# A transformer layer with FP4 feed-forward on one core: FP4 and layer norm in steps of different periods, and the queue's part between the two pairs of maxima

## The chip, the core and the metric

The kernel runs on one core of one Trainium2 chip. The metric is the device time of one execution in microseconds; of the kernel before, three executions took 3696.54, 3698.85 and 3699.21 us, median 3698.85. Five engines work side by side, each through its own instruction stream: TensorE (PE in the profile; PEld is its loading of weights), VectorE (DVE), ScalarE (ACT), GpSimd (POOL) and SyncE (SP), which in this kernel issues nearly all DMAs. They wait for each other through semaphores only.

## What is computed

A post-norm transformer layer over 4 batches of 2048 rows of 256 numbers: attention with 16 heads of 16, and a gated feed-forward of 704 columns whose linears take inputs and weights rounded to FP4 in blocks of 16.

```python
def fp4_quant_dequant(x):                  # blocks of 16 along the last dim
    scale = jnp.maximum(jnp.max(jnp.abs(xb), axis=-1, keepdims=True) / 6.0, 1e-12)
    idx = jnp.searchsorted(_MID, jnp.abs(xb / scale))
    return (_GRID[idx] * jnp.sign(xb) * scale).reshape(shape)
def fp4_linear(x, w):
    return jnp.einsum('bsk,nk->bsn', fp4_quant_dequant(x), fp4_quant_dequant(w))

scores = jnp.einsum('bhld,bhmd->bhlm', q, k) * SCALE
out = jnp.einsum('bhlm,bhmd->bhld', softmax(scores), v)      # then @ Wo.T
x = layernorm(x + attention(x))
h = silu(fp4_linear(x, w_gate)) * fp4_linear(x, w_up)
x = layernorm(x + fp4_linear(h, w_down))
```

## The kernel before

**Steps and periods.** The attention is cut into 64 steps, one for each batch `b`, block of 512 queries `qb` and group `g` of four heads (two pairs). A step has 16 periods, one for each 128 keys; the main loop (L700 to L736) runs over 1046 periods. Three steps are in the works at once: in one period, `maxima` (L382) makes the scores of one step for 128 queries against 512 keys, only to find each row's maximum; 20 periods later (`LEAD`) `exponentials` (L423) makes the transposed scores of that step again, the maxima subtracted inside the matmul, and takes the exponential; 2 periods after that (`LAG`) `values` (L434) multiplies by V.

**A period before, in TensorE's order:** two pairs of `pm` matmuls (one pair for each pair of heads; each fills one of two PSUM buffers of pool `ps_m`, and VectorE's `mx` reduction at L397 reads that buffer and frees it); two `pe` matmuls with two exponentials on ScalarE (L431); four `av`; the other two `pe` with their exponentials; at the end, `period(1)` (L654).

**The queue.** All other work is cut into parts by generators: a `yield` of 300 (`LEAST`) or more ends a part, of less it goes on. `period` first runs the steps that are due (`take_due`, L122), then one part of each generator in `urgent` (`max_rows`, which turns a finished step's maxima into rows for Q; `normalize`, which divides by the sums), and if none of these was a part, one part of `queue`. The queue holds the projections (`project`, L300: transposes of `xb`, then `pq` matmuls for K and Q, `pv` for V; order of the pieces at L666), the preparation of the weights (`prepare`, L232), and for each finished block of 512 queries a `chain` with the output projection and the feed-forward (L585), in which the next batch's projection (`other`) is threaded. PSUM for the parts and for `pe` comes in turn from the three banks of `ps_x`.

**A chain (four steps, 64 periods):** `residual` (four `py` parts, GpSimd adds, layer norm, FP4), seven parts of `other` (L596), transposes of the rounded rows (`ptq`), `gate(0)`, two of `other`, `gate(1)`, two, `gate(2)`, two (a gate is four parts: `pg`, `pu`, `pg`, `pu`, each product on GpSimd), `turned` for tiles 0 and 1 (transposes `pth` of the rounded `h`), `gate(3)`, the rest of `other`, `down` (eight parts `pz` in two tiles), layer norm of the output rows, `turned` for 2 and 3, `down`. In the last chain the gates of odd tiles run on VectorE. A generator whose input isn't ready yields `LEAST`, so its period has no part.

**FP4** (`fp4`, L145): VectorE takes each block's largest (`amax`, L149), the scale (`sc`, L151) and its reciprocal (`rs`, L153); GpSimd (or the engine given) makes `xn` (L155, L157). A period later, through `later`, VectorE makes the power of two (`m`, L161, L162), and GpSimd adds and takes it away again and multiplies by the scale (L163 to L165). **Layer norm** (L484): `st` and `mv` on VectorE for two row tiles (L489, L490), the rest on GpSimd (L492 to L497).

**What sets the order.** TensorE's instructions stay in the order written (`keep_in_program_order`). On the other engines a scheduler orders instructions as their data become ready, program order deciding among those that are; so VectorE's small instructions can stand in another place than where the code puts them.

**Loads.** `load_k` (L365) brings K tiles of 512 keys from DRAM into one of 20 buffers, each issued every four periods a step and more ahead; `xnh` has three buffers and holds Q, K, V weights at the start and later the FP4 values of `h`.

Of the kernel before, what the change touches and what calls it, by code (L numbers as in the profile page):

```python
# [73 lines left out]
def block_kernel(  # L74
# [36 lines left out]


    clock = {"now": 0}
    due = deque()

    def later(periods, step, rest=0):

        state = {"done": None}
        due.append((clock["now"] + periods, step, state))
        return lambda: state["done"] is not None and clock["now"] >= state["done"] + rest  # L120

    def take_due():  # L122
        clock["now"] += 1
        for _ in range(len(due)):
            at, step, state = due.popleft()
            if at > clock["now"]:
                due.append((at, step, state))
                continue
            step()
            state["done"] = clock["now"]  # L130


    def matmul(*args, **kw):
        tc.keep_in_program_order(nc.tensor.matmul(*args, **kw))  # L134
# [9 lines left out]

    def fp4(pool, t, tag, gain=1.0, engine=None):  # L145

        p, nb, _ = t.shape
        amax = pool.tile([p, nb], F32, tag="amax" + tag, name="amax")
        nc.vector.tensor_reduce(amax, t, AX.X, ALU.max, apply_absolute_value=True)  # L149
        sc = pool.tile([p, nb], F32, tag="sc" + tag, name="sc")  # L150
        nc.vector.tensor_scalar(sc, amax, gain / 6.0, 1e-12, ALU.mult, ALU.max)  # L151
        rs = pool.tile([p, nb], F32, tag="rs" + tag, name="rs")
        nc.vector.reciprocal(rs, sc)  # L153
        engine = engine or nc.gpsimd
        engine.tensor_scalar(rs, rs, gain * TIES_DOWN, 1.0, ALU.mult, ALU.mult)  # L155
        xn = pool.tile([p, nb, FB], F32, tag="xn" + tag, name="xn", bufs=3 if tag else 2)
        engine.tensor_tensor(xn, t, rs.unsqueeze(2).to_broadcast([p, nb, FB]), ALU.mult)  # L157

        def rounded():
            m = pool.tile([p, nb, FB], F32, tag="m" + tag, name="m", bufs=1)  # L160
            nc.vector.tensor_single_scalar(m.bitcast(I32), xn.bitcast(I32), EXPONENT, ALU.bitwise_and)  # L161
            nc.vector.tensor_scalar(m, m, 1.0, ROUND, ALU.max, ALU.mult)  # L162
            engine.tensor_tensor(xn, xn, m, ALU.add)  # L163
            engine.tensor_tensor(xn, xn, m, ALU.subtract)  # L164
            engine.tensor_tensor(xn, xn, sc.unsqueeze(2).to_broadcast([p, nb, FB]), ALU.mult)  # L165

        return xn, later(1, rounded, 4 if tag == "" else 2)

# [36 lines left out]
    for name, w in (("wk", wk), ("wq", wq), ("wv", wv)):  # L205
        loaded[name] = p2.tile([P, KC, D], F32, tag="xnh", name=name, bufs=3)
        nc.scalar.dma_start(loaded[name], w.rearrange("(c p) k -> p c k", p=P))
# [24 lines left out]
    def prepare():  # L232
# [12 lines left out]
        def load(w, i):  # L245
            if w is w_down:
                t = p2.tile([P, FF], F32, tag="wl", name="wl", bufs=1)
                nc.sync.dma_start(t, w[i * P : (i + 1) * P, :])
                return fp4(p2, t.rearrange("p (b f) -> p b f", f=FB), "h")
            t = p2.tile([RF, 2, D], F32, tag="wl", name="wl", bufs=1)  # L250
            nc.sync.dma_start(t, w[2 * i * RF : 2 * (i + 1) * RF, :].rearrange("(c p) k -> p c k", p=RF))
            return fp4(p2, t.rearrange("p c (b f) -> p (c b) f", f=FB), "")

        def transposed(w, i, q, done):
            while not done():
                yield LEAST
            if w is w_down:
                q = q.rearrange("p b f -> p (b f)")
# [41 lines left out]
    def project(b, tb, what):  # L300
# [7 lines left out]
        for kc in range(KC):  # L308
# [4 lines left out]
            yield 600  # L313
        for name, c in [(w[0], int(w[1])) for w in what if w != "v"]:
            w, dst = (wkT, kx[b % 2][c][:, :, rows]) if name == "k" else (wqT, qx[(b * NQB + tb) % len(qx)][c])
# [16 lines left out]
            projected.add((b, tb, name + str(c)))  # L332
        for t in range(QT if "v" in what else 0):
            v = vt[t // 2]
            pv = psum("pv")
            for kc in range(KC):
                matmul(
                    pv[:, :D], xT[:, kc, t * P : (t + 1) * P], wvT[:, kc, :], start=(kc == 0), stop=(kc == KC - 1)
                )
            src = pv[:, :D].rearrange("p (g i j d) -> p g i j d", g=NG, i=NP, j=2)  # L340
            for j in range(2):
                nc.scalar.copy(v[:, :, t % 2, :, 2 * j * DH : (2 * j + 1) * DH], src[:, :, :, j, :])
            if t % 2:
                t0 = tb * QT + t - 1
                for g in range(NG):
                    nc.sync.dma_start(vx[b % 2][g, :, t0 : t0 + 2, :], v[:, g].rearrange("p t i c -> p t (i c)"))
            if t == QT - 1:
                projected.add((b, tb, "v"))
            yield 900

# [14 lines left out]
    def load_k(s, kb):  # L365
        b, qb, g = steps[s]
        for i in range(NP):
            c, h = divmod(g * HG + i * 2, NC)
            k = p1.tile([P, QB], F32R, tag="k", name="k", bufs=20)
            for j in range(2):  # L370
                nc.sync.dma_start(
                    k[R * j : R * j + R, :].bitcast(F32), kx[b % 2][c][:, h + j, kb * QB : (kb + 1) * QB]
                )
            k_sb[s, i, kb] = k
# [108 lines left out]

    def layer_norm(r, t0, n):  # L484

        mv = p2.tile([P, n, 2], F32, tag="mv", name="mv")
        for t in range(n):
            st = p2.tile([P, 6], F32, tag="st", name="st")
            nc.vector.bn_stats(st, r[:, t0 + t, :])  # L489
            nc.vector.bn_aggr(mv[:, t, :], st)  # L490
        rstd = p2.tile([P, n], F32, tag="rstd", name="rstd")
        nc.gpsimd.tensor_scalar_add(rstd, mv[:, :, 1], LN_EPS)  # L492
        nc.gpsimd.tensor_tensor(rstd, rstd, minus_half[:, :n], ALU.pow)
        minus = p2.tile([P, n], F32, tag="minus", name="minus")
        nc.gpsimd.tensor_scalar(minus, mv[:, :, 0], -1.0, 1.0, ALU.mult, ALU.mult)
        for t in range(n):
            nc.gpsimd.tensor_scalar(  # L497
                r[:, t0 + t, :], r[:, t0 + t, :], minus[:, t : t + 1], rstd[:, t : t + 1], ALU.add, ALU.mult
            )

    def residual(b, qb, x1, xq):

        for t in range(QT):
# [10 lines left out]
            if t % 2:  # L514
                layer_norm(x1, t - 1, 2)
                tiles = x1[:, t - 1 : t + 1].rearrange("p t (b f) -> p (t b) f", f=FB)
                later(3, lambda tiles=tiles: xq.append(fp4(p2, tiles, "")))
            yield 900
# [35 lines left out]
    def turned(hq, tiles, hT):  # L554

        while not all(t in hq and hq[t][1]() for t in tiles):
            yield LEAST
        hq = [hq[t][0].rearrange("p b f -> p (b f)") for t in tiles]
        for t in range(2):
# [25 lines left out]
    def feed_forward(b, qb, between):  # L585
# [9 lines left out]
        other = projection(*between) if between is not None else iter([LEAST] * 6)  # L595
        yield from islice(other, 7)  # L596
        while len(xq) < QT // 2 or not all(done() for _, done in xq):
            yield LEAST
        xqT = p1.tile([P, KC, QB], F32, tag="xqT", name="xqT")
        for kc in range(KC):  # L600
            pt = psum("ptq")
            for t in range(QT):
                q = xq[t // 2][0].rearrange("p (t b) f -> p t (b f)", t=2)
                transpose(pt[:, t * P : (t + 1) * P], q[:, t % 2, kc * P : (kc + 1) * P], ident)
# [4 lines left out]
        def gate(t):  # L609
# [3 lines left out]
            yield from gated(xqT, h, t, engine)  # L613
            blocks = h.rearrange("p (b f) -> p b f", f=FB)
            later(1, lambda: hq.update({t: fp4(p2, blocks, "h", gain=0.5, engine=engine)}))

        def out_rows(t):
            layer_norm(x1, t, 2)
            at = slice(qb * QB + t * P, qb * QB + (t + 2) * P)
            nc.sync.dma_start(out[b, at, :].rearrange("(t p) d -> p t d", p=P), x1[:, t : t + 2, :])  # L620

# [4 lines left out]
        yield from gate(2)  # L626
        yield from islice(other, 2)
        hT = p2.tile([P, 2, NFC, P], F32, tag="hT", name="hT", bufs=1)
        yield from turned(hq, (0, 1), hT)
        yield from gate(3)  # L630
        yield from other
# [68 lines left out]
    for n in range(-LEAD, N + LAG):  # L700
# [10 lines left out]
        if n > 0 and kt % QT == 0:  # L711
            ahead, kb = divmod(n - QT + 2 * NKT, NKT)
            if ahead < len(steps):
# [6 lines left out]
                load_k(ahead, kb // QT)  # L720

        for i in range(NP):
            if m < N:
                maxima(sm, im, i)
        for i in range(NP):
            if 0 <= n < N:
# [5 lines left out]
        if n >= LAG and kv == NKT - 1:  # L732
            urgent.append(normalize(sv))
            if sv % NG == NG - 1:
                queue.append(chain(*steps[sv][:2]))
        period(1 if n >= 0 else 2)  # L736
    banks["more"] = True
# [37 lines left out]
```

## Time and profile before

| what | us |
|---|---|
| median of three executions | 3698.85 (3696.54 to 3699.21) |
| the profiled execution, its time | 3695.37 |
| its span in the profile | 3693.6 |
| TensorE busy | 3540.7 |
| VectorE busy (of it maxima, L397) | 2805.0 (2407.9) |
| ScalarE busy (of it exponentials, L431) | 2694.0 (2217.9) |
| GpSimd busy | 1293.4 |

The clock granted to TensorE was 0.982 of full speed over the whole span. By stretches, TensorE's busy time was:

| stretch, us | TensorE busy, us | of us |
|---|---|---|
| 0 to 100 | 63.01 | 100 |
| 100 to 330 | 201.05 | 230 |
| 330 to 500 | 168.14 | 170 |
| 500 to 3500 | 2963.06 | 3000 |
| 3500 to 3600 | 95.78 | 100 |
| 3600 to 3694 | 49.70 | 94 |

How the views below are read. In a line of the groups, after the bar stand busy time, mean nanoseconds of one, and after the second bar the engine's idle time just before those instructions with what ended it. A line of the waits says who waited for whom: microseconds in total, times, longest. A line of a timeline has start, duration, engine, line, operation, output and inputs with the shape, and in brackets the idle time just before it. A matmul is called by its output: `pm` are scores for maxima, `pe` for exponentials.

### The profile page before, as it was taken

To read this page: it belongs to the slowest core of one execution; us is meant where nothing else is said; L and a number is where in the kernel's file an instruction comes from. 1 tells how busy PE (TensorE), PEld (TensorE's weight loads), DVE (VectorE), ACT (ScalarE), POOL (GpSimd) and SP (SyncE) were. 2 spreads that over 40 slices of the span, in tenths; PEclk is the share of its full clock that TensorE was granted. 3 is DMA by queue.
4 is the path that set the end of the run, shared out by engine and by line. 5 is a ranking of instruction groups with operands and counts; after the bars stand their busy time and mean duration, and the time that the engine had idled before them with its cause. 6 is when DMAs were issued, how large, how long until landed. Compare 5 with 4: busy or idle time off the path is not lost.

```text
span 3693.6 us, 57860 instructions
## 1 busy us (share of the span) xinstructions
PE 3540.7 (96%) x21396; PEld 1602.0 (43%) x21396; DVE 2805.0 (76%) x3250; ACT 2694.0 (73%) x5452; POOL 1293.4 (35%) x1542
## 2 busy tenths in 40 slices
PE   5889999999999999999999999999999999999995
PEld 4433444444444444444444444444443434444343
DVE  3777777787787877878787787778778788878834
ACT  2667777777777777777777777777777777777772
POOL 0331432424243242423424243342424325241425
PEclk8899999999999999999999999999999999999997
DMA  6643333223232332323323232322322221222100
GB/s 217 188 137 117 93 91 105 81 85 115 68 114 84 94 94 85 109 70 109 95 78 106 85 97 88 97 89 74 113 75 63 75 79 57 75 68 86 47 7 6
DMA packets 197954, 334.18 MB, mean 90 GB/s; under 512 B 26024, under 2 KB 75560, under 8 KB 197672
## 3 DMA queue, kind: packets, MB, share of 16 engines
q1 hardware_dynamic: 196280, 329.16, 29.2%
q8 instruction: 171, 2.80, 0.3%
q10 hardware_dynamic: 1392, 1.31, 0.1%
q14 instruction: 111, 0.91, 0.1%
HBM read 242.81 MB, written 86.51 MB: 89 GB/s over the span
## 4 chain that ended last, share of the span: by engine, by line
PE 82%; DVE 11%; DMA 2%; POOL 2%; SPq 1%; issue 1%; ACT 1%; ACTq 0%; POOLq 0%; DVEq 0%
PE av L134 24%; PE pe L134 18%; PE pm L134 16%; DVE mx L397 8%; PE pz L134 5%; PE pg L134 5%; PE pu L134 5%; PE pq L134 3%; PE pth L137 1%; PE pv L134 1%; PE pa L137 1%; PE py L134 1%; PE pn L137 1%; DMA k<-kx 1%; DMA xb<-in_L_attn_x_dram 1%; DVE amax L149 1%
## 5 line engine op out<-in xcount | busy, mean ns | idle before, releaser
L397 DVE TENSOR_REDUCE mx<-pm 128x2 f32<-128x1024 f32 x2048 | 2407.9, 1217 | 706.8 <-PE pm L134 702.5
L431 ACT ACTIVATE e<-pe 128x512 f32<-128x512 f32 x4096 | 2217.9, 595 | 671.2 <-PE pe L134 666.0
L134 PE MATMUL av<-e,v 128*32 128x512 f32 x8192 | 1098.3, 608 | 0.0
L134 PE MATMUL pe<-q,k 64*128 64x512 f32 x4096 | 1037.2, 456 | 4.8 <-ACT e L431 4.4
L134 PEld LDWEIGHTS pe<-q,k 64*128 64x128 f32 x4096 | 476.4, 185 | 969.0 <-ACT e L431 855.7
L134 PE MATMUL pm<-k,q 62*128 62x512 f32 x4096 | 803.8, 448 | 60.0 <-DVE mx L397 53.0
L134 PEld LDWEIGHTS pm<-k,q 62*128 62x128 f32 x4096 | 347.0, 186 | 373.2 <-issue 178.6
L134 PEld LDWEIGHTS av<-e,v 128*32 128x32 f32 x8192 | 162.2, 108 | 332.2 <-issue 314.1
L537 POOL TENSOR_TENSOR a<-a,g 128x352 f32<-128x352 f32 x124 | 116.4, 939 | 499.5 <-ACT a L536 499.5
L582 POOL TENSOR_TENSOR x<-x,read 128x128 f32<-128x128 f32 x128 | 58.9, 460 | 493.6 <-ACT read L142 493.6
L134 PE MATMUL pz<-wdT,hT 128*128 128x128 f32 (+1 forms) x1536 | 230.0, 292 | 0.0
L163 POOL TENSOR_TENSOR xn<-xn,m 128x704 f32<-128x704 f32 (+2 forms) x104 | 159.5, 1534 | 157.7 <-DVE m L162 139.0
L134 PEld LDWEIGHTS pz<-wdT,hT 128*128 128x128 f32 (+1 forms) x1536 | 191.0, 191 | 45.5 <-ACT e L431 18.2
L551 POOL TENSOR_TENSOR h<-a,u 128x352 f32<-128x352 f32 x124 | 116.2, 937 | 226.7 <-ACT u L550 224.4
L134 PE MATMUL pg<-wgT,xqT 128*128 128x352 f32 x512 | 187.4, 489 | 0.0
L513 POOL TENSOR_TENSOR x<-x,read 128x256 f32<-128x256 f32 x64 | 46.7, 730 | 400.2 <-ACT read L142 399.9
L134 PE MATMUL pu<-wuT,xqT 128*128 128x352 f32 x512 | 186.1, 486 | 0.0
L164 POOL TENSOR_TENSOR xn<-xn,m 128x704 f32<-128x704 f32 (+2 forms) x104 | 159.8, 1536 | 5.6
L165 POOL TENSOR_TENSOR xn<-xn,sc 128x704 f32<-128x704 f32 (+2 forms) x104 | 131.5, 1264 | 7.8
L538 POOL TENSOR_TENSOR a<-a,g 128x352 f32<-128x352 f32 x124 | 118.8, 958 | 9.7
L134 PEld LDWEIGHTS pg<-wgT,xqT 128*128 128x128 f32 x512 | 88.3, 191 | 58.5 <-ACT e L431 19.1
L134 PEld LDWEIGHTS pu<-wuT,xqT 128*128 128x128 f32 x512 | 88.2, 191 | 58.7 <-ACT e L431 20.0
(95 smaller groups left out, 2283.1 us busy)
## 6 DMA issues: line engine op xcount, KB each, us to landing
k<-kx SPq DMA_DIRECT2D x1024, 128.0 KB
v<-vx SPq DMA_DIRECT2D x64, 768.0 KB
q<-qx SPq DMA_DIRECT2D x256, 124.0 KB
kx<-khi SPq DMA_DIRECT2D x64, 256.0 KB
qx<-qhi SPq DMA_DIRECT2D x64, 256.0 KB
xb<-in_L_attn_x_dram SPq DMA_DIRECT2D x27, 512.0 KB
vx<-vt SPq DMA_DIRECT2D x128, 96.0 KB
x<-in_L_attn_x_dram SPq DMA_DIRECT2D x16, 512.0 KB
```

The lines of the kernel that those rows point to most:

```text
L134: tc.keep_in_program_order(nc.tensor.matmul(*args, **kw))
L137: tc.keep_in_program_order(nc.tensor.transpose(*args))
L163: engine.tensor_tensor(xn, xn, m, ALU.add)
L164: engine.tensor_tensor(xn, xn, m, ALU.subtract)
L165: engine.tensor_tensor(xn, xn, sc.unsqueeze(2).to_broadcast([p, nb, FB]), ALU.mult)
L397: nc.vector.tensor_reduce(mx_sb[s][:, t, 2 * i : 2 * i + 2, kb], pm, AX.X, ALU.max)
L431: nc.scalar.activation(e, pe[j], AF.Exp, scale=SCALE)
L513: nc.gpsimd.tensor_add(x1[:, t, :], x1[:, t, :], read(py[:, :D]))
L537: engine.tensor_mul(a, a, g)
L538: engine.tensor_add(a, a, g)
L551: engine.tensor_mul(h[:, cols], a, u)
L582: nc.gpsimd.tensor_add(x1[:, t, cols], x1[:, t, cols], read(pz))
```

## The change

The part of the queue moves from the end of a period to between the two pairs of maxima; the normalisation's first instruction (a copy of the sums on ScalarE) is issued where the step ends, not by `period`.

```diff
         for i in range(NP):
             if m < N:
                 maxima(sm, im, i)
+            if i == 0:
+                period(1 if n >= 0 else 2)
...
         if n >= LAG and kv == NKT - 1:
-            urgent.append(normalize(sv))
+            heads = normalize(sv)
+            next(heads)
+            urgent.append(heads)
...
-        period(1 if n >= 0 else 2)
```

`later` takes several steps, each with its own number of periods; `fp4` and `layer_norm` are cut into such steps. For `h` and the rows of `x1` they are `largest` (after 2 or 3 periods), `scaled` (1 later), `power` (2 later), `rounded` (1 later). The weight pieces (`spread=False`) keep two steps.

```diff
-    def later(periods, step, rest=0):
+    def later(*steps, rest=0):
...
+        if spread:
+            done = later((wait, largest), (1, scaled), (2, power), (1, rounded), rest=3 if tag else 5)
+        else:
+            done = later(
+                (wait, lambda: (largest(), scaled())), (1, lambda: (power(), rounded())), rest=2 if tag else 4
+            )
+        return lambda: made[2], done
...
+        def moments(t):
             st = p2.tile([P, 6], F32, tag="st", name="st")
             nc.vector.bn_stats(st, r[:, t0 + t, :])
             nc.vector.bn_aggr(mv[:, t, :], st)
...
+        later(*[(1, lambda t=t: moments(t)) for t in range(n)], (0, normal))
```

`normal` holds the GpSimd half of the layer norm and then calls what follows it (the FP4 of the rows, or the store of the output).

In the chain, three gates stand together, and the projections' parts move:

```diff
-        yield from islice(other, 7)
+        yield from islice(other, 10)
...
         yield from gate(2)
-        yield from islice(other, 2)
+        yield from gate(3)
         hT = p2.tile([P, 2, NFC, P], F32, tag="hT", name="hT", bufs=1)
         yield from turned(hq, (0, 1), hT)
-        yield from gate(3)
         yield from other
```

`project` now takes its pieces in the order that is asked for, `k0, q0, v, k1, q1`; before, V's parts came after all of K's and Q's, whatever the order asked.

```diff
-        for name, c in [(w[0], int(w[1])) for w in what if w != "v"]:
+        def q_or_k(name, c):
...
-        for t in range(QT if "v" in what else 0):
+        def values_of():
+            for t in range(QT):
...
+        for w in what:
+            yield from values_of() if w == "v" else q_or_k(w[0], int(w[1]))
```

Buffers: `k` 20 to 16, `xnh` (and `xn` of `h`) 3 to 4.

## The prediction

> **What bounds the kernel now.** I read the page first: engine shares, then the chain of work that ended last, then the costliest groups.
>
> ```profile
> span 3693.6 us, 57860 instructions
> PE 3540.7 (96%) x21396; PEld 1602.0 (43%) x21396; DVE 2805.0 (76%) x3250; ACT 2694.0 (73%) x5452; POOL 1293.4 (35%) x1542
> PE 82%; DVE 11%; DMA 2%; POOL 2%; SPq 1%; issue 1%; ACT 1%; ACTq 0%; POOLq 0%; DVEq 0%
> L397 DVE TENSOR_REDUCE mx<-pm 128x2 f32<-128x1024 f32 x2048 | 2407.9, 1217 | 706.8 <-PE pm L134 702.5
> L134 PE MATMUL pm<-k,q 62*128 62x512 f32 x4096 | 803.8, 448 | 60.0 <-DVE mx L397 53.0
> ```
>
> TensorE is the bound, and 11% of the chain is VectorE, nearly all of it the row maxima. The last line says where VectorE makes TensorE wait: the score matmuls `pm` idled 53.0 us, because the PSUM buffer they wanted was still being read. Next the waits between 500 and 3500 us, the even middle of the run (13 chains of some 230 us each):
>
> ```profile
> PE pm L134 <- DVE mx L397: 35.8, 82, 0.8
> PEld pm L134 <- DVE mx L397: 134.0, 332, 1.2
> ```
>
> The weight loads (PEld) run beside matmuls, so the first line is what costs time: 35.8 / 13 = 2.75 us a chain. The same view over seven stretches of 400 us from 500 to 3300 gives 3.9, 3.9, 2.9, 2.9, 3.9, 6.0 and 8.1. Now the timeline of one such place, VectorE and then TensorE:
>
> ```profile
> 1915.13 0.43 DVE L489 BATCH_NORM_STATS2 st<-x 128x6 f32<-128x256 f32 x1 [0.22 <-POOL x L513]
> 1915.47 0.67 DVE L149 TENSOR_REDUCE amax<-x 128x32 f32<-128x512 f32 x1
> 1916.06 0.17 DVE L490 BATCH_NORM_AGGREGATE mv<-st 128x2 f32<-128x6 f32 x1
> 1916.18 0.61 DVE L151 TENSOR_SCALAR sc<-amax 128x32 f32<-128x32 f32 x1
> 1916.82 0.35 DVE L153 RECIPROCAL rs<-sc 128x32 f32<-128x32 f32 x1
> 1917.09 0.37 DVE L489 BATCH_NORM_STATS2 st<-x 128x6 f32<-128x256 f32 x1
> 1917.37 1.20 DVE L397 TENSOR_REDUCE mx<-pm 128x2 f32<-128x1024 f32 x1
> ```
> ```profile
> 1918.63 0.50 PE L134 MATMUL pm<-k,q 62*128 62x512 f32 x2 [0.25 <-DVE mx L397]
> 1919.83 0.50 PE L134 MATMUL pm<-k,q 62*128 62x512 f32 x2 [0.69 <-DVE mx L397]
> ```
>
> Six small instructions of layer norm and FP4 stand in front of one maximum from 1915.13 to 1917.37, and TensorE loses 0.25 + 0.69 us. In this chain (1900 to 2129 us) there are three more, at 2106.4, 2109.1 and 2117.6 (0.35, 0.26, 0.39), where the output rows' layer norm falls into periods that have no part of the queue. Everything else in the chain is matmuls back to back.
>
> **The change, part by part.** Sums are made against the profiled execution, 3695.37 us; the median of the runs is 3698.85, so I add 3.5 at the end.
>
> *The part between the two pairs of maxima.* In a period before, the second pair of `pm` starts about 0.335 us after the first, and each pair's buffer is freed by its maximum about 0.55 us (matmul and start) plus 1.217 us later, or 1.217 more for the second. So the second pair of the next period finds its buffer free if the period is longer than 0.55 + 2.43 − 0.335 = 2.65 us plus the small VectorE work put before it. With the part between, each pair only waits for its own maximum, and the bound is 0.55 + 1.217 = 1.77 us plus that work. In the 3.1 us periods of transposes the allowance rises from about 0.45 to 1.3 us; in periods without a part (2.2 to 2.4 us) nothing can stand between, and nothing is gained. TensorE's own work is the same in another order; periods with nothing late last 3.70 (pg, pu), 3.38 (pq, py, pv) and 2.90 us (transposes) in the timeline, and I leave them there: 0.
>
> *FP4 and layer norm in steps.* No instruction is added or taken away. A pair of row tiles costs VectorE 2 × (0.414 + 0.177) + 0.672 + 0.369 + 0.350 + 0.444 + 0.420 = 3.44 us, an `h` tile 0.876 + 0.187 + 0.428 + 0.579 + 0.608 = 2.68, by their groups' means. A period of 3.38 us has 3.38 − 2.43 = 0.95 us over for it. The program order spreads these over 5 periods or more instead of 2; but the emitted order, in which VectorE takes what is ready, still has `amax`, `sc` and `rs` of `h` in one gap (1.49 us), with the two `m` steps one or two gaps later, and the residual's pieces in gaps of up to four instructions (1.1 to 1.4 us) where six stood together (2.6). By sites of a chain: residual 0.94 → about 0.5 (two gaps still fill the allowance, so the backlog survives one maximum); output rows' norm 1.0 → about 0.5 (fewer empty periods there, three in a row elsewhere with nothing but maxima); new, 0.5 for gate 2 and gate 3 back to back, where `amax`, `sc`, `rs` and the `m` pair of one tile follow those of the next within six periods. The 2.75 of a chain become about 1.5: 16 × 1.25 = −20. Bounds: all of it gone, 16 × 2.75 = −44, with 0.1 us for the next `pe` matmul at each of some 100 stalls −54; at the other end +10, from this row:
>
> ```profile
> L162 DVE TENSOR_SCALAR m<-m x82: 414/527/1150, 527.4 to 3476.2; 128x704 f32<-128x704 f32 x54, 128x512 f32<-128x512 f32 x28
> ```
>
> The same step takes 0.53 us (median) or up to 1.15. The long ones run beside a GpSimd instruction. Gate 3 now follows gate 2, so GpSimd's `a` and `h` products of gate 3 (0.94 us each) lie where gate 2's `m` steps are: 0.6 us on each of two steps in 16 chains would be +19, and most of it inside the allowance. I take +4, so the steady part is −16.
>
> The Trainium skill ("SBUF — State Buffer", "Who interferes with whom") speaks against this edit: VectorE and GpSimd share a port pair that one holds for a whole instruction, and reductions never contend. That fits this row, and the maxima, which hold 1.21 us beside GpSimd. By its rule every `m` step that meets a product would wait, the steady part would be about −1, and the sum some 15 us higher; by the row, most steps meet none.
>
> *The order of the chain's pieces, V ahead of k1, ten parts ahead instead of seven.* The same parts in other periods. V's copies and its DMAs to `vx` are issued some 20 periods earlier on ScalarE and SyncE, k1's and q1's `kx`/`qx` stores later; all are read a batch later (more than 64 periods), so they are hidden by that lead: 0. If it were gone, a load of 13 us (the longest `k` in the trace) would show once a batch, +40.
>
> *`k` buffers 20 → 16, `xnh` 3 → 4, maxima's row sums and the normalisation a part earlier or later.* A `k` load may now start 4 periods later, and is needed 8 periods × 3.5 = 28 us after it can start; the longest took 13.2 us: 0. If the lead were gone, those behind it on SyncE (`q`, `v`, `x1`) would be late next. The pn part gets its rows 0.33 us later against a lead of 2 us to the next step's exponentials: 0.
>
> *Start-up (100 to 330 us).* TensorE is busy 201 of 230 us there; the idle 29 is `xb`, `k` and weight loads on SyncE and three weight pieces' FP4. The weight pieces keep two steps (`spread=False`) but move in the emitted order; three `amax` stand closer together behind DMAs whose longest waits were 8.2, 6.4 and 6.2 us. One such wait met or avoided is ±8: I take 0 ± 8.
>
> *The tail.* After the last attention period only the last chain's feed-forward is left:
>
> ```profile
> 3648.43 0.66 PE L137 MATMUL pth<-ident,xn 128*128 128x128 f32 x4 [3.99 <-POOL xn L165]
> 3658.67 1.94 PE L137 MATMUL pth<-ident,xn 128*128 128x128 f32 x8 [9.58 <-DVE xn L165]
> 3677.08 1.97 PE L137 MATMUL pth<-ident,xn 128*128 128x128 f32 x8 [3.16 <-DVE xn L165]
> ```
>
> Before, gate 3's matmuls come after the 9.58 us wait for tile 1, and its products on VectorE (3663.92 to 3669.67) and FP4 (3669.71 to 3677.02) after those. Now gate 3's four parts run inside that wait; the emitted VectorE order puts its products from about 3657.7, between tile 1's last steps, and its FP4 from about 3662.5. It is done near 3670; tile 2's FP4 on GpSimd slips by 2 us to 3669. The last transposes start near 3670.5 instead of 3677.08: −6.5. Bounds −3 (tile 1 pushed back further) and −8 (the whole shift of the products, with the 3.16 us gone).
>
> Sum: −16 − 6.5 + 0 = −22.5. 3695.4 − 22.5 + 3.5 = 3676.
>
> **The rivals.**
> *A: the stalls only change place.* The emitted order keeps FP4's first three steps together, and the two-buffer wait returns a pair later. For it: `amax`, `sc`, `rs` in one gap in nearly every tile. Against it: the allowance is 0.85 us larger whatever the bunch. Steady 0 to −4, tail −6.5: about 3690.
>
> *B: slower; ScalarE gets the part's copies too late.* ScalarE in a gate period:
>
> ```profile
> 1974.52 0.45 ACT L534 COPY g<-pg 128x352 f32<-128x352 f32 x1 [0.35 <-PE pg L134]
> 1974.87 0.47 ACT L536 ACTIVATE a<-pg 128x352 f32<-128x352 f32 x1
> 1975.36 1.08 ACT L431 ACTIVATE e<-pe 128x512 f32<-128x512 f32 x2
> ```
>
> The exponentials already follow the copies without a gap. With a pair of maxima ahead of the part, the copies come 0.335 us later and the exponentials with them; the second `pe` pair (1976.26) then has its third buffer, first exponential ended near 1976.2, with some 0.25 us to spare. It decides once more than that is used up. There are 256 parts with two copies (128 pg, 128 pq); at 0.1 to 0.33 us each +26 to +84, say 0.2: +51 − 22.5 gives 3727. Against: the period's ScalarE load is 4 × 0.595 + 0.92 = 3.3 of 3.70 us, so the 0.335 is caught up in the same period.
>
> *C: all of it.* The allowance covers every bunch: −54 − 6.5: about 3638 at best, 3648 with 10 us left.
>
> **How the numbers follow.** Forecast 0.58, A 0.16, B 0.18, C 0.08. The forecast's own bounds are 3698.85 − 35 − 8 − 8 = 3648 with nearly full relief and, with the contention, 3698 at worst; the range to hold 8 in 10 takes in A, C and the mild end of B: 3648 to 3708. Some 0.2% (7.4 us) is what a measurement of this kernel can tell from no change. Faster (below 3691.5): the forecast nearly whole, C, and a part of A: 0.64. Within: the rest of A and some of the forecast and B: 0.19. Slower: most of B: 0.17.
>
> **What would show it.** Right: `pm` idle for `mx` between 500 and 3500 us falls from 35.8 to about 20; periods of pg stay at 3.70 us; the last transposes wait for 3670, not 3677; `m` keeps its 0.53 median. Wrong: pg or pq periods longer by 0.1 or more with `pe` waiting for `e` (B); `pm` idle unchanged (A); a new wait of TensorE for `k`, `xb` or `wl` at any place; `m` steps of gate 2 at 1.1 us with `pm` waiting behind them.

## The result, and the profile after

The changed kernel takes 3715.62 us (median of five, 3713.84 to 3719.02) against 3697.65 for the kernel before: ratio 1.005, interval 1.0035 to 1.0064. I had forecast 3676, with a range of 3648 to 3708. The profiled execution took 3714.04 us against 3695.37, spans 3712.3 and 3693.6; the difference to be explained is 18.7 us of span.

The page of the changed kernel: span, engines, chain of work that ended last, maxima, score matmuls.

```profile
span 3712.3 us, 57994 instructions
PE 3541.8 (95%) x21396; PEld 1538.3 (41%) x21396; DVE 2848.2 (77%) x3250; ACT 2686.0 (72%) x5452; POOL 1293.3 (35%) x1542
PE 82%; DVE 8%; POOL 3%; DMA 2%; issue 2%; ACT 2%; SPq 0%; POOLq 0%; ACTq 0%
L424 DVE TENSOR_REDUCE mx<-pm 128x2 f32<-128x1024 f32 x2048 | 2455.2, 1218 | 668.8 <-PE pm L137 571.8
L137 PE MATMUL pm<-k,q 62*128 62x512 f32 x4096 | 933.9, 446 | 50.2 <-DVE mx L424 42.6
```

TensorE runs the same instructions. VectorE's share of the chain has fallen from 11% to 8% and `pm`'s idle time for `mx` from 53.0 to 42.6 us, as the change intends; ScalarE's has risen from 1% to 2%, GpSimd's from 2% to 3%. (`pm`'s busy time rises from 803.8 to 933.9 because its two pairs no longer overlap; a period with `pg` and nothing late is 3.70 us in both.)

To place the loss I took the start of the first `pm` of chosen periods in both traces, counting periods from the first maxima on (a chain of four steps is 64 periods):

| stretch | changed less before, us |
|---|---|
| start to period 90 | +9.9 |
| period 90 to 154 | +1.4 |
| period 154 to 794, ten chains | +13.2 (1.32 a chain) |
| period 794 to 1023 | −7.3 |
| to the last transposes `pr` | +4.0 |
| the tail after them | −2.6 |

A chain is 218.6 us long in the kernel before, and the ten chains of one trace agree with each other to some 0.3 us, so the third row is firm; the first, which hangs on when loads land, comes from one execution of each kernel. Of the −7.3, 1.0 lie in the three chains to period 986 and 6.3 in the last 37 periods, from which 8 gate matmuls, 12 transposes `pth` and 11 `pz` have moved behind period 1023: part of it is work put off, and comes back as the +4.0.

TensorE's waits between 500 and 3500 us (who waits for whom: us in total, times, longest) say what is new in them; its first four lines:

```profile
PE pm L137 <- DVE mx L424: 22.1, 40, 0.9
PE pth L140 <- ACT e L458: 5.3, 11, 0.5
PE pg L137 <- ACT e L458: 5.0, 13, 0.4
PE pv L137 <- ACT e L458: 3.8, 10, 0.4
```

The first line was 35.8; the other three did not exist: 34 waits of some 0.41 us, each at the part that follows a `pa` part, in the ten chains three to a chain. (Below them stand 3 more such waits at `pz`, 1.2 us, and 1.8 us of `pe` waiting for `e`.) One of them, VectorE and then TensorE:

```profile
2018.68 1.23 DVE L424 TENSOR_REDUCE mx<-pm 128x2 f32<-128x1024 f32 x1 [0.68 <-PE pm L137]
2019.82 0.25 DVE L487 RECIPROCAL rd<-pa 128x16 f32<-128x16 f32 x1
2019.99 1.16 DVE L424 TENSOR_REDUCE mx<-pm 128x2 f32<-128x1024 f32 x1
2021.07 0.47 DVE L492 TENSOR_TENSOR oq<-pa,rd 128x128 f32<-128x128 f32 x2
```
```profile
2018.57 0.66 PE L140 MATMUL pa<-ident,av_sb 128*128 128x128 f32 x4
2021.33 0.46 PE L137 MATMUL pm<-k,q 62*128 62x512 f32 x2
2022.18 1.45 PE L137 MATMUL pg<-wgT,xqT 128*128 128x352 f32 x4 [0.39 <-ACT e L458]
```

And the same place in the kernel before, VectorE:

```profile
2005.79 0.26 DVE L460 RECIPROCAL rd<-pa 128x16 f32<-128x16 f32 x1
2006.08 0.49 DVE L465 TENSOR_TENSOR oq<-pa,rd 128x128 f32<-128x128 f32 x2
2006.49 2.35 DVE L397 TENSOR_REDUCE mx<-pm 128x2 f32<-128x1024 f32 x2
```

Before, `rd` and both `oq` read the `pa` bank in one go, and it is free about 1.5 us after the transposes begin. Now the period's second pair of `pm` comes right after `pa`, and its maximum goes between `rd` and `oq`: the bank is held for 3 us. Of the three banks that the parts and `pe` share, two are left. In the instructions of the trace the wait for VectorE's last read of `pa` stands at the third request for a bank after it in the kernel before, at the sixth in the changed one; so the fifth, the next part's, has to wait until ScalarE has emptied a bank filled 0.7 us earlier.

The second new place comes once a chain, where gate 3 follows gate 2 (VectorE, then TensorE):

```profile
2057.08 1.25 DVE L171 TENSOR_SCALAR m<-xn 128x704 int32<-128x704 int32 x1 [0.74 <-POOL xn L166]
2058.25 1.21 DVE L424 TENSOR_REDUCE mx<-pm 128x2 f32<-128x1024 f32 x1
```
```profile
2059.51 0.50 PE L137 MATMUL pm<-k,q 62*128 62x512 f32 x2 [0.90 <-DVE mx L424]
```

`m` waits 0.74 us for GpSimd, then takes 1.25 us instead of 0.5 beside it, and the maximum behind it keeps `pm` waiting 0.90 us.

### The profile page after: what moved, and what is told of

It reads as the page before. It is cut to its first block, busy times and chain, and to the rows that moved or that the text cites. A ratio compares the mean times of both kernels' runs of the same rounds, so it can differ in the third digit from the quotient of the medians.

```text
span 3712.3 us, 57994 instructions
## 1 busy us (share of the span) xinstructions
PE 3541.8 (95%) x21396; PEld 1538.3 (41%) x21396; DVE 2848.2 (77%) x3250; ACT 2686.0 (72%) x5452; POOL 1293.3 (35%) x1542
## 4 chain that ended last, share of the span: by engine, by line
PE 82%; DVE 8%; POOL 3%; DMA 2%; issue 2%; ACT 2%; SPq 0%; POOLq 0%; ACTq 0%
PE av L137 24%; PE pe L137 19%; PE pm L137 15%; PE pz L137 5%; DVE mx L424 5%; PE pu L137 4%; PE pg L137 4%; PE pq L137 3%; PE pv L137 2%; PE pth L140 1%; ACT e L458 1%; PE pa L140 1%; PE py L137 1%; PE pn L140 1%; POOL xn L166 1%
## 5 line engine op out<-in xcount | busy, mean ns | idle before, releaser
L424 DVE TENSOR_REDUCE mx<-pm 128x2 f32<-128x1024 f32 x2048 | 2455.2, 1218 | 668.8 <-PE pm L137 571.8
L137 PE MATMUL pe<-q,k 64*128 64x512 f32 x4096 | 1048.2, 457 | 7.0 <-ACT e L458 3.6
L137 PE MATMUL pm<-k,q 62*128 62x512 f32 x4096 | 933.9, 446 | 50.2 <-DVE mx L424 42.6
L137 PEld LDWEIGHTS pm<-k,q 62*128 62x128 f32 x4096 | 412.1, 186 | 342.2 <-DVE mx L424 199.3
L145 ACT COPY read<-pz 128x128 f32<-128x128 f32 x128 | 34.1, 266 | 122.5 <-PE pm L137 103.9
L566 ACT COPY g<-pg 128x352 f32<-128x352 f32 x128 | 58.0, 453 | 88.5 <-PE pg L137 80.7
```

What stands on the lines that cost most here:

```text
L424: nc.vector.tensor_reduce(mx_sb[s][:, t, 2 * i : 2 * i + 2, kb], pm, AX.X, ALU.max)
L566: nc.scalar.copy(g, pg[:, :FH])
```

## The experiments

Differences below are to the kernel before, in us; "a chain" is the mean of the ten from period 154 to 794, and "held" steps are pinned to the order in which they are written (part 5). `pm` idle stands twice: between 500 and 3500 us, and in the ten chains alone. The spans and the columns behind them are of one execution of each kernel, and executions of one kernel differ by several us (e6: 3686.07 to 3697.13); the ratios are of all.

| kernel | span | at period 90 | a chain | `pm` idle for `mx`, 500 to 3500 | in the ten chains | ratio (interval) |
|---|---|---|---|---|---|---|
| before | 3693.6 | 0 | 0 | 35.8 | 19.4 | 1 |
| changed | 3712.3 | +9.9 | +1.32 | 22.1 | 11.1 | 1.005 (1.0035 to 1.0064) |
| e1 part at the end | 3713.4 | +5.5 | +2.13 | 52.5 | 35.7 | 1.0051 (1.0036 to 1.0066) |
| e2 part in the middle alone | 3714.1 | +4.7 | +0.82 | 18.6 | 2.2 | 1.0054 (1.0039 to 1.0069) |
| e3 oq first | 3694.4 | +8.1 | −0.07 | 22.3 | 11.2 | 0.9992 (0.9983 to 1.0001) |
| e4 buffers alone | 3692.2 | −0.7 | +0.01 | 35.9 | 19.4 | 0.999 (0.998 to 0.9999) |
| e5 e3, part at the end to period 90 | 3694.9 | +8.0 | −0.05 | 21.9 | 11.3 | 0.9995 (0.9985 to 1.0005) |
| e6 e3, weights' first step at once | 3687.5 | +1.3 | −0.06 | 22.2 | 11.2 | 0.9984 (0.9975 to 0.9993) |
| e7 e3, m steps a period later | 3696.2 | +10.8 | −0.13 | 22.5 | 11.2 | 0.9994 (0.9985 to 1.0003) |
| e8 e2 with oq first | 3691.2 | +3.1 | −0.70 | 19.3 | 2.2 | 0.9986 (0.9977 to 0.9995) |
| e9 e6, steps held | 3667.4 | +2.3 | −1.51 | 11.2 | 0 | 0.9929 (0.9915 to 0.9942) |
| e10 steps held, part at the end | 3664.6 | −1.9 | −1.49 | 23.2 | 7.1 | 0.9924 (0.9912 to 0.9937) |
| e11 before, its steps held | 3706.0 | +1.9 | +0.38 | 52.5 | 25.0 | 1.0029 (1.0017 to 1.0041) |
| e12 changed, steps held | 3689.2 | +7.9 | −0.19 | 8.6 | 0 | 0.9986 (0.9976 to 0.9995) |

**1. One part of the change undone, or done alone.** e1 takes the part back to the end of the period (the normalisation is started by the period again), e2 puts only the part's new place, with the normalisation's first copy, into the kernel before, e4 only the buffers.

```diff
             if m < N:
                 maxima(sm, im, i)
-            if i == 0:
-                period(1 if n >= 0 else 2)
...
+        period(1 if n >= 0 else 2)
```

> The changed kernel with the part put back to the end of the period (and the normalisation started by the period again); the steps, the order of the chain and the buffers stay. Theory A, the part's place is what costs (3714 for the changed kernel, 3695 before, both profiled): the waits of pth, pg and pv on ScalarE's exponentials after each pa part (1.26 us in one chain, about 19 us over the run) go, and pm waits for mx rise back towards the 36 us of before between 500 and 3500 us; profiled time 3690 to 3702. Rival B, the steps and the chain's order cost: the time stays at 3710 to 3716. Start-up: if the part's place put the xb load behind others, the first pair of period 90 comes within 3 us of the kernel before (371.6 us), otherwise some 10 us later, as in the changed kernel.

> The kernel before with nothing but the part between the two pairs of maxima (and the normalisation's copy issued with it). Theory A: the pa sites appear here too, and with them +1.2 us in each chain, 3705 to 3720. Rival B: the gain of the wider allowance shows alone, 3675 to 3692, and the loss came with the steps and the order of the chain.

> The kernel before with k at 16 buffers and xnh at 4, nothing else. My prediction costs it at nothing: 3693 to 3698. If the later k loads are what puts xb late in the start-up, it is 3702 to 3708, with the loss before 372 us.

Both halves cost 20 us alone, and together no more. For e1 that is the time of the rival, not of theory A, although the waits after `pa` that A named are gone. e2 has the waits after `pa` (its view has 16.0 us of them in `pg`, `pz` and `pth`) beside the fall of `pm`'s idle time. e1 has none of them, but its `pm` idles more than before:

```profile
PE pm L137 <- DVE mx L424: 52.5, 112, 0.7
```

So the part's place is one cause, and the steps or the chain's order another that the part's place hides. The buffers cost nothing, as predicted. (At period 90 e1 is 5.5 us late, between the two cases that its expectation named; part 3 takes this up.)

**2. The held bank.** e3 pins the two `oq` behind `rd` and the next maximum behind them; e8 does the same to e2.

```diff
-        nc.vector.tensor_reduce(mx_sb[s][:, t, 2 * i : 2 * i + 2, kb], pm, AX.X, ALU.max)
+        largest = nc.vector.tensor_reduce(mx_sb[s][:, t, 2 * i : 2 * i + 2, kb], pm, AX.X, ALU.max)
+        if pinned:
+            pinned.pop()
+            tc.keep_in_program_order(largest)
...
         for i in range(NP):
-            nc.vector.tensor_tensor(
+            rows = nc.vector.tensor_tensor(
...
+            tc.keep_in_program_order(rows)
+        pinned.append(s)
```

> The changed kernel with the two oq multiplies pinned behind rd, and the next maximum behind them, so that VectorE reads the pa bank in one go. If the held PSUM bank is the cause of the waits after pa, these (14 us between 500 and 3500 us, some 17 to 19 over the run) go and the profiled time is 3695 to 3698; the maximum held back by 0.8 us lies inside the allowance. If the wait comes from the exponentials being late for another reason, nothing changes: 3712 to 3716.

> The kernel before with the part in the middle and oq first, nothing else (the same without oq first had a span of 3714.1, with 16 us of waits after pa and 18.6 us of pm for mx between 500 and 3500 us). What the wider allowance is worth by itself: by my prediction's size 0.9 us a chain, 3680 to 3686; if the idle of pm stood beside ScalarE's own limit and was not worth its length, 3691 to 3698.

17.9 us of span go, and with them every wait for ScalarE at those parts. VectorE at a `pa` part in e3, and what is left of the view of the waits:

```profile
2007.73 0.25 DVE L490 RECIPROCAL rd<-pa 128x16 f32<-128x16 f32 x1
2008.01 0.49 DVE L495 TENSOR_TENSOR oq<-pa,rd 128x128 f32<-128x128 f32 x2
2008.41 2.50 DVE L424 TENSOR_REDUCE mx<-pm 128x2 f32<-128x1024 f32 x2
```

```profile
PE pm L137 <- DVE mx L424: 22.3, 40, 0.9
PE pg L137 <- DVE oq L495: 1.7, 3, 0.6
PE pe L137 <- DMA q<-nr: 0.6, 2, 0.4
```

This settles the loss in the ten chains: 1.32 becomes −0.07. But `pm` idles 8.2 us less in them than in the kernel before, and they are only 0.7 us shorter. e8 shows what the wider allowance brings by itself: 0.70 a chain, a little short of the 0.9 named, while its span of 3691.2 falls into the other range: it loses 3.1 us by period 90, and behind period 794 it gains nothing. So the steps and the chain's order give 0.6 a chain back, and the periods say which. At the residual, periods 542 to 545 of one chain last 13.73 us in e8 and 13.76 in e3: the steps bring nothing there. At gate 3 behind gate 2, which e8 does not have, period 578 lasts 3.82 us in e3, 0.72 more than in e9 (part 5), which has the same order of the chain and holds its steps: that is what the new order costs with `m` where the scheduler puts it.

**3. The start-up.** e5 and e6 start from e3. e5 has the part at the end of the period up to period 90; e6 has this:

```diff
-            done = later(
-                (wait, lambda: (largest(), scaled())), (1, lambda: (power(), rounded())), rest=2 if tag else 4
-            )
+            largest()
+            scaled()
+            done = later((1, lambda: (power(), rounded())), rest=2 if tag else 4)
```

> The kernel with oq first (3694.4 us of span, 8.1 us behind the kernel before at the first maxima of period 90), with the part at the end of the period up to period 90 and in the middle from there on. If the part's place costs the start-up, the 8.1 falls to 3 or less and the span to 3687 to 3690; if the weight pieces' later first step costs it, it stays at 5 to 8 and 3692 to 3695 (the kernel with the part at the end everywhere stands 5.5 behind there).

> The kernel with oq first, with the weight pieces' amax, sc and rs issued at once when the piece is loaded, as in the kernel before, and the rest one period later. If the later first step costs the start-up, the 8.1 us at period 90 falls to 4 or less and the span to 3689 to 3691; if the part's place does, it stays at 7 to 9, span 3694.

The weights' first step it is: 6.8 of e3's 8.1 us at period 90 in these traces, and e6's span lies just below the range named. (The medians of e3, e5 and e6, 3695.68, 3696.60 and 3692.31, differ by less, 3.4 and 4.3 us, so the size is uncertain.) In the changed kernel that step is issued a period after the load, and each following piece, which needs the one buffer `wl`, comes later. TensorE's long waits there, and the first of them in the kernel before:

```profile
143.20 1.08 PE L140 MATMUL ptx<-ident,xb 128*128 128x128 f32 x4 [16.49 <-DMA xb<-in_L_attn_x_dram]
203.54 0.80 PE L137 MATMUL pm<-k,q 62*128 62x512 f32 x2 [5.94 <-DVE mx L424]
267.86 0.80 PE L137 MATMUL pm<-k,q 62*128 62x512 f32 x2 [7.64 <-DVE mx L424]
```
```profile
140.18 1.09 PE L137 MATMUL ptx<-ident,xb 128*128 128x128 f32 x4 [6.01 <-DMA xb<-in_L_attn_x_dram]
```

The two at `pm` are maxima behind an `amax` that waits for its weight piece's DMA; VectorE waits for such pieces 35.0 us in all, 22.8 before. The first, 16.49 us, is not what it seems: TensorE comes there some 7.5 us earlier than before (126.7 against 134.2), and the wait ends 3.0 us later. It does make period 25 late, by 6.6 us in the changed kernel and 7.0 in e6; but e6, which keeps a wait of 16.0 us, makes up most of that and is 1.3 us late at period 90. e5 takes this loss away (it is on time at period 35) and is 8.0 us late at period 90 all the same. The two losses do not simply add: with the old first step the part's new place alone costs 4.7 us at period 90 in e2 and 3.1 in e8, and the new first step with the part at the end 5.5 in e1. How they combine, no run here separates.

**4. The m steps a period later.**

```diff
-            done = later((wait, largest), (1, scaled), (2, power), (1, rounded), rest=3 if tag else 5)
+            done = later((wait, largest), (1, scaled), (3 if tag else 2, power), (1, rounded), rest=3 if tag else 5)
```

> The kernel with oq first, with the m steps of h three periods after the scale instead of two, so that GpSimd has a period more to make xn between gate 3's products. If the maximum held behind m (0.90 us of pm idle once a chain, at gate 2 and gate 3) is a wait for GpSimd, it goes in all chains: pm idle for mx between 500 and 3500 us falls from 22 to about 10 us, and the span from 3694.4 to 3681 to 3686. If m then only stands before another maximum, it stays within 3 us of 3694.

Nothing was gained, and this was the useful miss: the emitted VectorE order around gate 3 has `m` before the same maximum as without the edit. The scheduler did not put the small instruction in the period it is written in. It is the same at the residual, where the changed kernel's order is that of e8, which doesn't have these steps.

**5. The order held.** e9 pins each of the small instructions (`amax`, `sc`, `rs`, both `m`, `st`, `mv`) behind the VectorE instruction written before it, on top of e6; e10 has the same pins and weights' first step with the part at the end and `oq` left to the scheduler; e12 only the pins in the changed kernel; e11 pins the two-step FP4 and the layer norm of the kernel before.

```diff
+        stay = tc.keep_in_program_order if spread else (lambda op: op)
...
-            nc.vector.tensor_reduce(amax, t, AX.X, ALU.max, apply_absolute_value=True)
+            stay(nc.vector.tensor_reduce(amax, t, AX.X, ALU.max, apply_absolute_value=True))
...
```

> The kernel with oq first and the weights' first step at once (span 3687.5), with every step of FP4 and layer norm pinned behind the VectorE instruction written before it, so that the steps stand in the periods they are written in. In that kernel the emitted order ignores the steps (the residual's small instructions stand as they do without them, and m waits for GpSimd in front of a maximum once a chain). If the spreading is worth what I forecast for it, pm idle for mx between 500 and 3500 us falls from 22 to 8 or less and the span to 3668 to 3676; if the bunches cost little beyond what shows in one place, 3683 to 3688.

> The same pinned steps and weights with the part at the end of the period, oq left to the scheduler. It tells the pinned steps from the part's place: with the part at the end and the steps not held (span 3713.4) pm idled 52.5 us for mx between 500 and 3500 us, 2.1 to 2.3 us more a chain than before. If that came from the unheld steps, it falls below 25 us and the span to 3677 to 3690; if it came from the chain's order and the small allowance, it stays above 40 us and 3700 to 3712.

> The kernel before with its own FP4 and layer norm instructions (not the weights') pinned behind the VectorE instruction written before them, nothing else. The steps stay two, so amax, sc and rs of a tile still stand together. If the order alone, without more steps, brings the gain of the pinned steps, the span falls to 3670 to 3678; if it takes steps that are cut and held, it stays within 12 us of 3693.6.

> The changed kernel with its steps pinned and nothing else: oq is left to the scheduler and the weights' first step stays late. If the three causes add up (steps not held 20 us, pa's bank 18 us, the weights' first step 7 us between the kernels that differ in one of them), the span is 3712.3 less 20, 3690 to 3695, with the waits after pa still there (13 to 17 us between 500 and 3500 us). If the pinned steps also cure the wait after pa, 3672 to 3677.

e9 is 26.2 us of span shorter than the kernel before, just better than the range named, though `pm` idles 11.2 us and not 8 or less. Its VectorE timeline at the residual's FP4:

```profile
1918.32 0.68 DVE L157 TENSOR_REDUCE amax<-x 128x32 f32<-128x512 f32 x1
1918.92 1.22 DVE L425 TENSOR_REDUCE mx<-pm 128x2 f32<-128x1024 f32 x1
1920.58 1.23 DVE L425 TENSOR_REDUCE mx<-pm 128x2 f32<-128x1024 f32 x1 [0.45 <-PE pm L137]
1921.72 0.17 DVE L162 TENSOR_SCALAR sc<-amax 128x32 f32<-128x32 f32 x1
1921.80 1.22 DVE L425 TENSOR_REDUCE mx<-pm 128x2 f32<-128x1024 f32 x1
1922.94 0.34 DVE L164 RECIPROCAL rs<-sc 128x32 f32<-128x32 f32 x1
1923.67 1.23 DVE L425 TENSOR_REDUCE mx<-pm 128x2 f32<-128x1024 f32 x1 [0.40 <-PE pm L137]
```

One small instruction stands between two maxima, and VectorE waits for TensorE again. In the chain from period 538 the periods of e3 sum to 218.51 us and those of e9 to 217.07. Of the 1.44, 0.76 lie in periods 542 to 544 (3.26, 3.52, 3.56 become 3.09, 3.09, 3.40), where the residual's bunch is, and 0.72 in period 578 (3.82 becomes 3.10), where `m` waited for GpSimd; the rest is −0.04. In the ten chains e9 shows no `pm` idle at all.

e12 keeps the wait after `pa`:

```profile
PE pm L137 <- DVE mx L425: 8.6, 27, 0.7
PE pth L140 <- ACT e L459: 5.3, 11, 0.5
PE pg L137 <- ACT e L459: 5.0, 13, 0.4
PE pv L137 <- ACT e L459: 3.9, 10, 0.4
```

Its span of 3689.2 lies just below what was expected: the pins take 23.1 us from the changed kernel, 20.1 from e6 to e9, so the three causes nearly add up; its ten chains are 13.2 us longer than e9's and show 12.6 us of waits after `pa`. e11 shows that holding is not enough: with two steps a tile, `pm` idles 52.5 us, and it is slower than before by 12.4 us of span, just outside what was expected. e10 shows that with steps cut and held the part's place is worth nothing in the chains (−1.49 and −1.51), although `pm` idles 7.1 us there in e10 and not at all in e9; its span is 12 us below the range named for it. Its start-up is 4.2 us better, which makes e10 the fastest by 2.8 us of span; its median of 3669.81 and e9's of 3670.41 cannot be told apart.

## Why the prediction was wrong

**The step that failed first** is the one on the part between the pairs: "TensorE's own work is the same in another order; periods with nothing late ... I leave them there: 0". TensorE's work is the same. But a part's PSUM bank is emptied by another engine, and I counted only the maxima's buffers when the order of VectorE changed around it. The second pair's maximum came between `pa`'s two readers, and the next part paid some 0.4 us, three times a chain: 1.39 us a chain (1.32 to −0.07 with oq first), 17.9 us in all. Neither my sum nor a rival had it. Rival B looked for a late bank at the right engine, at the wrong parts: periods with `pg` stayed at 3.70 us except after `pa`.

**The steps, −16 predicted.** With the bank's wait out of the way, the wider allowance, the steps and the chain's order together brought 0.07 a chain, against 0.70 for the allowance alone. e3 is 5.1 us ahead of the kernel before from period 154 to the last transposes, and some of that is work put off. The failing step is "residual 0.94 → about 0.5 ... The 2.75 of a chain become about 1.5". I had read the emitted order, and had seen that `amax`, `sc` and `rs` still stand in one gap, and credited the spreading all the same; rival A ("the emitted order keeps FP4's first three steps together") was the right reading of this part.

The sum itself was wrong before any run. 3000 us hold 13.7 chains of 218.6 us, not 13, and they are not alike: `pm` idles 1.94 us a chain in the ten, which is what the sites add up to (0.25 + 0.69 + 0.35 + 0.26 + 0.39), and 12.1 us in the three from period 794 to 986. What I expected to be left at the sites, 1.5, belongs to the 1.94. Set against the average of 2.75 it gave 1.25 a chain, 20 us; by the sites it is 0.44 a chain, 7 us. That e9 and e10 bring 1.51 and 1.49, near the 1.25, is luck: in e9 nothing is left of the idle time, where the forecast had more than half of it left, and e10 gets there without the wider allowance.

**`pm` idle as a price.** I forecast a fall from 35.8 to about 20, and it fell to 22.1. It did not buy what I priced it at. In the ten chains e3 has 8.2 us less of it than the kernel before and gains 0.7; e8 17.2 less and gains 7.0; e9 19.4 less and gains 15.1; e10 12.3 less and gains 15.0. Part of the lost time is not in the line. At the residual e3 loses 0.76 us to e9 and shows 0.23 as `pm` idle; matmul by matmul nearly all of it lies at four starts of `pm` (0.17, 0.11, 0.39, 0.10), and what the line leaves out is hidden under the time that the view gives to the matmul before. Why the 7.1 us of idle in e10 cost it nothing against e9, no run shows.

**GpSimd beside `m`**, +4 predicted. The place was right, the size 0.72 a chain (period 578, e3 against e9), some 11 us; from the timeline 0.74 us of it is a wait for GpSimd's `xn` and 0.75 the longer `m`, so the wait, which I did not price, is as large as the contention.

**Start-up, 0 ± 8**: +9.9. The item named ("The weight pieces ... move in the emitted order") is the cause of most of it, 6.8 us from e3 to e6 in one trace each, 3.4 by the medians; the sign was not in the trace of before, but the delay of the first step by a period was in the diff, and I should have put it on the side of loss.

**The tail, −6.5**: −2.6, after +4.0 in the last attention periods, where more parts of the last chain but one are left than before. Tile 3's `amax` came where I put it (3683.89, 21.3 us later than 3662.6 as everything there), but its FP4 took 11.9 us instead of 7.3. VectorE, then TensorE:

```profile
3683.89 0.88 DVE L156 TENSOR_REDUCE amax<-h 128x44 f32<-128x704 f32 x1
3686.08 1.27 DVE L164 TENSOR_SCALAR rs<-rs 128x44 f32<-128x44 f32 x1
3690.25 0.43 DVE L517 BATCH_NORM_STATS2 st<-x 128x6 f32<-128x256 f32 x1 [1.98 <-POOL x L614]
3690.60 1.35 DVE L171 TENSOR_SCALAR m<-xn 128x704 int32<-128x704 int32 x1
```
```profile
3695.90 1.94 PE L140 MATMUL pth<-ident,xn 128*128 128x128 f32 x8 [3.37 <-DVE mv L518]
```

Beside tile 2's FP4 on GpSimd, `rs` took 1.27 us and `m` 1.35, and a layer norm step that waits 1.98 us for GpSimd stands before `m`. The bound of −3 named a push-back, of the wrong tile.

**Right:** the `k` and `xnh` buffers at nothing (e4: no later than before in the chains, −1.4 at the end), gates at 3.70 us, and the median of `m` (0.52 and 0.51 us). V ahead of k1 and ten parts ahead instead of seven were not tried alone, nor was the chain's new order without the steps; the 0 for them is not shown.

## What to carry to other kernels

When work is moved between two users of a ring of buffers, list every buffer that is open across the move and who empties it, not only the ring that the move is meant to relieve. Steps written for different periods are steps only if the engine's emitted order keeps them there: compare that order with and without the edit before pricing it, and hold it where it doesn't. An idle line tells where to look; its length was not the time to be gained here, and an average of it over unlike stretches is no price for any of them.

## What the runs showed of the hardware

```profile
L171 DVE TENSOR_SCALAR m<-xn x82: 407/518/1250, 517.6 to 3458.3; 128x704 int32<-128x704 int32 x54, 128x512 int32<-128x512 int32 x28
3685.64 1.67 POOL L177 TENSOR_TENSOR xn<-xn,m 128x704 f32<-128x704 f32 x1 [0.53 <-DVE sc L161]
```
```profile
3671.31 0.18 DVE L155 TENSOR_SCALAR rs<-rs 128x44 f32<-128x44 f32 x1
```

The first two lines are of the changed kernel, the third of the one before. An `m` step of 704 columns took 1.25 us on VectorE beside GpSimd and some 0.5 without. `rs` of 44 columns, 0.18 us alone, took 1.27 us, and ended at 3687.35, when GpSimd's instruction beside it, begun 0.44 us before it, ended too (3687.31): here a short instruction was stretched as far as a long one. The maxima held 1.22 us in the kernels before and after. I had not expected a 0.2 us instruction to cost a microsecond. The Trainium skill ("SBUF — State Buffer", "Who interferes with whom") says that a VectorE instruction in one of its two-port modes and one of GpSimd contend for a shared port pair, that whichever issues first holds it for its whole instruction, and that `tensor_reduce` on this chip never contends: the stretched `rs` and `m` beside instructions of GpSimd and the steady maxima agree with it; that the port is what held them, no run here shows.
